# A small product of zeros in each half step of layer 0's attention

## The chip, the cores and the metric

The kernel runs on one core of one Trainium2 chip. Its time is device microseconds of one execution, from the first to the last instruction of the core and what lies around them; lower is better. Times named here are the medians of several runs.

## The reference

Two transformer layers over one sequence of 2048 tokens with 128 channels, in float32. Each layer is a modulated layer norm, attention, a modulated layer norm and a feed-forward part, with gated residuals. Only layer 0's attention is touched by the change:

```python
NHEADS, DK = 16, 8
q = (x @ Wq.T + bq).reshape(b, s, NHEADS, DK)
k = (x @ Wk.T + bk).reshape(b, s, NHEADS, DK)
v = (x @ Wv.T + bv).reshape(b, s, NHEADS, DV)
w = jnp.einsum('bshd,bzhd->bhsz', q, k)
w = w / jnp.sqrt(jnp.float32(DV))
w = jax.nn.softmax(w, axis=-1)
vw = jnp.einsum('bhsz,bzhd->bshd', w, v)
out = vw.reshape(b, s, NHEADS * DV) @ Wo.T + bo
```

There is no mask: every query sees all 2048 keys, in 16 heads of 8 channels. After it come layer 0's experts, layer 1's causal attention, and layer 1's feed-forward part.

## The kernel before

**Units.** Queries are cut into four blocks of 512 (`QB`), keys into 16 tiles of 128, heads into four groups of four (`HG`). A unit is one block of queries with one group of heads: 16 units in layer 0. A bank of PSUM, `av`, holds a unit's weighted sums: 32 partitions for each of the four heads, 512 queries along the row.

**First pass: the maxima.** Softmax needs each query's largest score ahead of the exponential. `first_pass` computes scores with queries on the partitions (L379, a pair of products for two heads, 64 rows of queries and keys split into a high and a low part), and VectorE reduces them to maxima (L383). 32 such steps make a unit. `largest` joins them (L394), splits them in two parts (L404, L405), and `turn` transposes them (L412) and sends them by DMA into spare rows of the query stack.

**Second pass: the exponentials and the weighted sum.** `score` computes the scores again, with keys on the partitions and with the maximum already taken off (L444: the maxima sit in rows of the query stack, which is what `fused` means); ScalarE makes the exponential of two heads at a time (L454), and `weigh` multiplies it with the values (L470: four products, one for each head, in float32, so that each leaves two records in the profile). A unit has 32 half steps, two for each tile of keys: one half step computes scores for two of the four heads, and the weighted sums of half of the queries for all four heads of the tile before.

**Order.** The half steps are written as a generator, `steps`: scores, then `yield`, then one weighted sum. At the `yield` the caller, `look_ahead`, puts in one step of the first pass of the next unit, eight steps (`LEAD`) further ahead. So PE's stream in a half step is: a pair of shifted scores (L444), a pair of scores for the maxima (L379), one weighted sum (L470). `weighing` is the number of the unit whose weighted sum was written last; `other_bank` gives small products the bank that is not in use for it. Instructions are then placed by a scheduler, which may move them within their dependencies unless `keep_in_program_order` holds them.

**Buffers.** Both kinds of scores take their PSUM from one pool, `ps_s`, with three buffers of two banks. They come in turn: an L379 takes the buffer that the exponential of the half step before has read, an L444 the one that a maximum has read. The exponentials lie in five buffers, `ep`.

**Tile forms.** PE's array can be used in parts. The profile shows the part as rows x columns of the weights: 64*128 for L444 and L379, whose two products lie in the upper and the lower 64 rows; 128*32 for L470, whose four lie side by side; 128*128 for transposes and the rest. A float32r product leaves one record, a float32 product two.

Names that the steps use: L501 transposes a unit's sums at its end (`divide`), L528 copies them, L714 and L735 are small products of the expert routing with 16 columns, L230 transposes a layer norm, L450 is layer 1's product that subtracts the maxima (layer 1 is not `fused`), L160 copies a constant at the start.

Of the kernel before, what the change touches and what calls it, by code (L numbers as in the profile page):

```python
# [11 lines left out]
F32R = mybir.dt.float32r  # L12
# [7 lines left out]
P = 128  # L20
# [12 lines left out]
W = 32  # L33
HG = P // W
RT = 64
# [8 lines left out]
def two_layers(ctx: ExitStack, tc: tile.TileContext, a: dict, out: bass.AP):  # L44
    nc = tc.nc
    const = ctx.enter_context(tc.tile_pool(name="const", bufs=1))
# [94 lines left out]
    nc.gpsimd.memset(zeros, 0.0)  # L141
    blank = const.tile([P, P], F32, name="blank")
    nc.gpsimd.memset(blank, 0.0)


    iota = const.tile([P, 32], F32, name="iota")
# [140 lines left out]
    def attention(layer, hT, ngrp, dk, scale, causal, kvp, begin, prepare, wq, bq, folded, ended,  # L287
# [18 lines left out]
        fused = step > 4  # L306
# [4 lines left out]
        with ExitStack() as s:  # L311
# [8 lines left out]
            weighing = -1  # L320
# [105 lines left out]
            def second_pass(u):  # L426


                b, grp = units[u]
                nk = TB * (b + 1) if causal else NT  # L430
                av = banks[u % 2]
                held = {}

                def first_query(kt):
                    return (kt - TB * b) * P if causal and kt >= TB * b else 0

                def score(kt, pair):
                    own = causal and kt >= TB * b
                    q0 = first_query(kt)
                    ps = ps_s.tile([P, 2, QB], F32, name=f"{L}p2_{u}_{kt}_{pair}", tag="s")  # L440
                    for j in range(2):
                        g = 2 * pair + j
                        st, r = grp * nst + g // S, RT * (g % S)
                        nc.tensor.matmul(ps[:, j, q0:], kS(st)[r:r + RT, kt * P:(kt + 1) * P],  # L444
                                         qS[b][r:r + RT, st, q0:], start=True, stop=fused)
                    assert u in shift
                    for j in range(0 if fused else 2):
                        g = 2 * pair + j
                        r = RT * (g % S)
                        nc.tensor.matmul(ps[:, j, q0:], ones[r:r + RT, g // S, :],  # L450
                                         shift[u][r:r + RT, q0:],
                                         start=False, stop=True)
                    e = ep.tile([P, 2, QB], F32, name=f"{L}e_{u}_{kt}_{pair}", tag="e")
                    nc.scalar.activation(e[:, :, q0:], ps[:, :, q0:], AF.Exp, scale=scale)  # L454
                    if own:

                        nc.gpsimd.affine_select(  # L457
                            out=e[:, :, q0:q0 + P], in_=e[:, :, q0:q0 + P],
                            compare_op=ALU.is_ge, fill=0.0, base=0,
                            pattern=[[0, 2], [1, P]], channel_multiplier=-1)  # L460
                    held[kt, pair] = e

                def weigh(kt, c0, c1):
                    nonlocal weighing
                    weighing = u
                    c0 = max(c0, first_query(kt))
                    for g in range(HG):
                        if c0 < c1:

                            nc.tensor.matmul(av[g * W:(g + 1) * W, c0:c1], vA(kt, grp * HG + g),  # L470
                                             held[kt, g // 2][:, g % 2, c0:c1],
                                             start=(kt == 0 and c0 == 0), stop=(kt == nk - 1),
                                             skip_group_check=True)

                def steps():
                    for kt in range(nk):
                        for half in range(2):
                            score(kt, 1 - half)
                            yield
                            if len(weights) > lag:  # L480
                                weights.pop(0)()
                        for half in range(2):
                            weights.append(lambda kt=kt, half=half: weigh(
                                kt, half * QB // 2, (half + 1) * QB // 2))
                    last = weights.pop()
                    weights.append(lambda: (last(), late.extend(normalise(u, av))))

                return steps()

            def normalise(u, av):  # L490
# [717 lines left out]
```

## Time and profile before

| | us |
|---|---|
| median of 3 runs | 1276.62 (1274.73 to 1278.80) |
| the profiled execution | 1279.47 |
| its span, first to last instruction | 1277.8 |
| layer 0's attention, first to last L444 | 91.9 to 815.4 |
| PE, DVE, ACT, POOL busy, of the span | 91%, 74%, 61%, 7% |
| mean granted clock of PE | 0.936 |

PE is TensorE's matmuls, PEld its weight loads, DVE VectorE, ACT ScalarE, POOL GpSimd, SP SyncE. `out<-in` are the program's names of what an instruction writes and reads, then come sizes; xN is the number of instructions joined in a line. In a timeline the first number is the start, the second the duration, in microseconds. The ends of matmuls are modelled, and matmuls overlap in the array, so the time that one of them takes is better read from the starts of two that follow each other than from its duration. A wait is written as who waited, for whom, and then microseconds in total, times, and the longest.

### The profile page before, as it was taken

How to read it: one execution, taken by the hardware profiler on the slowest of the kernel's cores; microseconds unless marked ns; L12 is line 12 of the kernel's file. 1: busy time of each engine (PE TensorE's matmuls, PEld its weight loads, DVE VectorE, ACT ScalarE, POOL GpSimd, SP SyncE). 2: the span in 40 equal slices, each digit the busy share in tenths (PEclk: the TensorE clock that was granted, in tenths of full speed). 3: DMA queues.
4: the chain of work that ended last, by engine and by line, in shares of the span. 5: the costliest groups of instructions: out<-in, count | busy, mean ns of one | idle time of the engine just before them, and what ended most of it. 6: DMA issues, size and time to landing. Idle time of an engine off the chain costs nothing.

```text
span 1277.8 us, 22384 instructions
## 1 busy us (share of the span) xinstructions
PE 1166.8 (91%) x9230; PEld 525.9 (41%) x9230; DVE 946.8 (74%) x1495; ACT 773.1 (61%) x843; POOL 95.2 (7%) x157
## 2 busy tenths in 40 slices
PE   4579999999999999999999999879668999999985
PEld 3233443443344344334344434457433444444432
DVE  4788888889889898988998971342466769888225
ACT  6117777777777777777777777513114435656763
POOL 2011000000000000000000001210411011100113
PEclk9659999999999999999999999979966779999998
DMA  4831010213122024010000000231201101000001
GB/s 127 110 43 34 3 51 6 63 37 106 28 68 68 1 53 115 21 32 2 2 2 2 2 2 9 75 96 52 60 5 33 34 1 34 1 2 1 1 2 33
DMA packets 63095, 45.22 MB, mean 35 GB/s; under 512 B 6609, under 2 KB 56913, under 8 KB 62481
## 3 DMA queue, kind: packets, MB, share of 16 engines
q1 hardware_dynamic: 60224, 40.37, 12.8%
q10 hardware_dynamic: 1744, 1.32, 0.6%
q0 software_dynamic: 1024, 2.10, 0.5%
q8 instruction: 73, 1.20, 0.4%
q14 instruction: 30, 0.24, 0.1%
HBM read 9.88 MB, written 21.95 MB: 25 GB/s over the span
## 4 chain that ended last, share of the span: by engine, by line
PE 80%; DVE 11%; ACT 4%; issue 2%; DMA 1%; POOL 1%; another core or an unknown queue 0%; POOLq 0%; SPq 0%; DVEq 0%; ACTq 0%
PE a0bank L470 23%; PE a0p L444 17%; PE a0p L379 12%; PE a1bank L470 6%; PE a1p L444 4%; DVE a0mx L383 3%; PE a1p L379 2%; PE a1p L450 2%; DVE a1masked L388 2%; DVE a1mx L383 2%; PE sg L941 2%; ACT a0e L454 1%; PE gu L1007 1%; PE a0bank L501 1%; PE a0bank L412 1%
## 5 line engine op out<-in xcount | busy, mean ns | idle before, releaser
L383 DVE TENSOR_REDUCE a0mx<-a0p 128x2 f32<-128x1024 f32 x512 | 623.8, 1224 | 77.3 <-PE a0p L379 67.2
L454 ACT ACTIVATE a0e<-a0p 128x1024 f32<-128x1024 f32 x512 | 522.1, 1024 | 172.9 <-PE a0p L444 148.6
L470 PE MATMUL a0bank<-a0e,vA 128*32 128x256 f32 x4096 | 333.4, 391 | 0.5 <-ACT a0e L454 0.5
L379 PE MATMUL a0p<-kS,a0qS 64*128 64x512 f32 x1024 | 248.1, 481 | 25.9 <-DVE a0mx L383 13.4
L444 PE MATMUL a0p<-a0qS,kS 64*128 64x512 f32 x1024 | 260.7, 498 | 0.0
L454 ACT ACTIVATE a1e<-a1p 128x1024 f32<-128x1024 f32 (+3 forms) x160 | 143.1, 896 | 99.0 <-PE a1p L450 95.7
L444 PEld LDWEIGHTS a0p<-a0qS,kS 64*128 64x128 f32 x1024 | 97.3, 184 | 204.5 <-issue 131.9
L379 PEld LDWEIGHTS a0p<-kS,a0qS 64*128 64x128 f32 x1024 | 100.3, 192 | 110.8 <-ACT a0e L454 56.8
L470 PEld LDWEIGHTS a0bank<-a0e,vA 128*32 128x32 f32 x4096 | 86.4, 108 | 137.6 <-issue 124.4
L383 DVE TENSOR_REDUCE a1mx<-a1p 128x2 f32<-128x1024 f32 x96 | 115.7, 1221 | 29.0 <-PE a1p L379 28.1
L470 PE MATMUL a1bank<-a1e,vA 128*32 128x256 f32 (+1 forms) x1152 | 102.4, 388 | 2.3 <-POOL a1e L457 2.0
L444 PE MATMUL a1p<-a1qS,kS 64*128 64x512 f32 (+3 forms) x320 | 77.1, 474 | 2.5 <-DVE a1mx L388 0.9
L379 PE MATMUL a1p<-kS,a1qS 64*128 64x512 f32 (+3 forms) x320 | 68.5, 432 | 10.3 <-DVE a1mx L388 6.2
L388 DVE CUSTOM_DVE_ANT_0 a1masked<-a1p,later 128x128 f32<-128x128 f32 (+3 forms) x128 | 62.5, 488 | 13.7 <-PE a1p L379 8.7
L759 POOL DMA_INDIRECT sent<-hs,row_i x16 | 16.2, 1011 | 719.2 <-DVE ln11xn L223 689.6
L450 PE MATMUL a1p<-a1mT,a1ones 64*128 64x512 f32 (+3 forms) x320 | 62.6, 384 | 0.7 <-issue 0.7
L444 PEld LDWEIGHTS a1p<-a1qS,kS 64*128 64x128 f32 x320 | 31.8, 193 | 62.6 <-issue 33.4
L379 PEld LDWEIGHTS a1p<-kS,a1qS 64*128 64x128 f32 x320 | 33.1, 204 | 38.8 <-DVE a1mx L388 14.1
L457 POOL TENSOR_SCALAR_AFFINE_SELECT a1e<-a1e 128x256 f32<-128x256 f32 x64 | 26.3, 411 | 253.7 <-ACT a1e L454 253.7
L470 PEld LDWEIGHTS a1bank<-a1e,vA 128*32 128x32 f32 x1152 | 26.3, 109 | 46.0 <-issue 33.3
L413 ACT CAST a0mT<-a0bank 8x512 fp32r<-8x512 f32 x16 | 9.2, 574 | 45.4 <-PE a0bank L412 45.4
L450 PEld LDWEIGHTS a1p<-a1mT,a1ones 64*128 64x128 f32 x320 | 32.7, 199 | 2.3 <-issue 1.8
(342 smaller groups left out, 717.3 us busy)
## 6 DMA issues: line engine op xcount, KB each, us to landing
sent<-blank SPq DMA_DIRECT2D x68, 256.0 KB
kS<-a0qS SPq DMA_DIRECT2D x28, 128.0 KB
wgu_sb<-in_gate_up SPq DMA_DIRECT2D x1, 2048.0 KB
a0qS<-a0qh SPq DMA_DIRECT2D x62, 32.0 KB
a0qS<-a0ql SPq DMA_DIRECT2D x62, 32.0 KB
xs<-sent SPq DMA_DIRECT2D x31, 64.0 KB
y_rows<-y SPq DMA_DIRECT2D x7, 256.0 KB
a1qS<-a1qh SPq DMA_DIRECT2D x24, 64.0 KB
```

Source lines behind the costliest of these rows:

```text
L379: nc.tensor.matmul(ps[:, j, :n], qS[b][r:r + RT, st, i * P:(i + 1) * P], kS(st)[r:r + RT, kb * QB:kb * QB + n], start=True, stop=True)
L383: nc.vector.tensor_reduce(pm[:, i, 2 * pair:2 * pair + 2, kb], ps, AX.X, ALU.max)
L388: nc.vector.tensor_tensor_reduce(masked[:, :n], ps[:, j, :n], later[:, QB - n:], 1.0, LOWEST, ALU.add, ALU.max, pm[:, i, g, kb:kb + 1])
L412: nc.tensor.transpose(ps[:, i * P:(i + 1) * P], nm[:, i, :], ident)
L444: nc.tensor.matmul(ps[:, j, q0:], kS(st)[r:r + RT, kt * P:(kt + 1) * P], qS[b][r:r + RT, st, q0:], start=True, stop=fused)
L450: nc.tensor.matmul(ps[:, j, q0:], ones[r:r + RT, g // S, :], shift[u][r:r + RT, q0:], start=False, stop=True)
L454: nc.scalar.activation(e[:, :, q0:], ps[:, :, q0:], AF.Exp, scale=scale)
L457: nc.gpsimd.affine_select(out=e[:, :, q0:q0 + P], in_=e[:, :, q0:q0 + P], compare_op=ALU.is_ge, fill=0.0, base=0, pattern=[[0, 2], [1, P]] ...
L470: nc.tensor.matmul(av[g * W:(g + 1) * W, c0:c1], vA(kt, grp * HG + g), held[kt, g // 2][:, g % 2, c0:c1], start=(kt == 0 and c0 == 0), sto ...
L501: nc.tensor.transpose(ps[:, i * P:(i + 1) * P], o[:, i * P:(i + 1) * P], ident)
L759: nc.gpsimd.indirect_dma_start(out=sent[t], in_=hs[:, i, :], in_offset=None, out_offset=bass.IndirectOffsetOnAxis(ap=row_i.bitcast(U32)[:, ...
L941: nc.tensor.matmul(ps[:, j, :], w[:, k * P:(k + 1) * P], hT[:, b * QB:(b + 1) * QB], start=True, stop=True)
```

## The change

A constant of zeros, `nothing_r`, 64 x 32, is made at the start. In layer 0 (`fused`), once the unit's first weighted sum has been written (`weighing == u`), each half step adds one product behind the shifted scores: zeros as weights (64 rows, 32 columns), 128 keys of the first stack as the moving side, added to the first 32 partitions and 128 columns of the unit's bank `av`. It adds zero to sums that are being built. `keep_in_program_order` is put around it. Nothing reads it but the sums themselves.

```diff
@@ -141,6 +141,8 @@
     blank = const.tile([P, P], F32, name="blank")
     nc.gpsimd.memset(blank, 0.0)
+    nothing_r = const.tile([RT, W], F32R, name="nothing_r")
+    nc.scalar.copy(nothing_r, blank[:RT, :W])
@@ -476,6 +478,12 @@
                     for kt in range(nk):
                         for half in range(2):
                             score(kt, 1 - half)
+                            if fused and weighing == u:
+                                tc.keep_in_program_order(nc.tensor.matmul(
+                                    av[:W, :P], nothing_r, kS(0)[:RT, :P], start=False,
+                                    stop=False, skip_group_check=True))
                             yield
                             if len(weights) > lag:
                                 weights.pop(0)()
```

With it the lines of the changed kernel stand two further down up to the second edit, and eight further down behind it: L379, L444, L454 and L470 become L381, L446, L456 and L472, and the added product is L484.

## The prediction

> **What bounds the kernel now.** I read the page first, then one table of windows, then PE's timeline for three half steps, then the waits. The page says where the time is:
>
> ```profile
> PE 1166.8 (91%) x9230; PEld 525.9 (41%) x9230; DVE 946.8 (74%) x1495; ACT 773.1 (61%) x843; POOL 95.2 (7%) x157
> ...
> PE 80%; DVE 11%; ACT 4%; issue 2%; DMA 1%; POOL 1%; another core or an unknown queue 0%; POOLq 0%; SPq 0%; DVEq 0%; ACTq 0%
> ```
>
> PE carries 80% of the chain that ended last. The table of windows narrows this to layer 0's attention (first number: PE busy of 600 us; later 1.00: the granted clock):
>
> ```profile
> 100.00:700.00 600.00, 595.35 (x5243) 241.53 (x5236) 537.31 (x559) 448.44 (x457) 1.09 (x1) 1.00 0.13 37
> ```
>
> PE shows 99%, DVE 90%, ACT 75%, and the clock is granted in full, so the change can win no clock there. But ends of matmuls are modelled; what PE's time consists of is read from the starts. Three half steps on PE (start, duration, line, tile form, xcount):
>
> ```profile
> 500.04 0.50 PE L444 MATMUL a0p<-a0qS,kS 64*128 64x512 f32 x2
> 500.37 0.44 PE L379 MATMUL a0p<-kS,a0qS 64*128 64x512 f32 x2
> 500.74 0.64 PE L470 MATMUL a0bank<-a0e,vA 128*32 128x256 f32 x8
> 501.31 0.50 PE L444 MATMUL a0p<-a0qS,kS 64*128 64x512 f32 x2
> 501.72 0.50 PE L379 MATMUL a0p<-kS,a0qS 64*128 64x512 f32 x2
> 502.15 0.64 PE L470 MATMUL a0bank<-a0e,vA 128*32 128x256 f32 x8
> 502.72 0.50 PE L444 MATMUL a0p<-a0qS,kS 64*128 64x512 f32 x2
> 503.06 0.39 PE L379 MATMUL a0p<-kS,a0qS 64*128 64x512 f32 x2
> 503.38 0.42 PE L470 MATMUL a0bank<-a0e,vA 128*32 128x256 f32 x4
> ```
>
> A half step is one pair of shifted scores (L444), one pair of scores for the maxima (L379), one weighted sum (L470: four products, eight records, two passes). From start to start: L444 to L379 0.33, 0.41, 0.34; L379 to L470 0.37, 0.43, 0.32; L470 to the next L444 0.57 always. So a half step takes 1.23 to 1.27 us when nothing is waited for and 1.41 otherwise. Over all of layer 0 the trace's PE starts give the same in the mean: L444 to L379 391 ns (459 of them, one stall of 2.2 us left out), L379 to L470 384 ns, L470 to L444 571 ns. The two groups of quick and slow steps have a cause:
>
> ```profile
> PEld a0p L379 <- ACT a0e L454: 56.8, 219, 0.7
> ```
>
> In 219 half steps the weight load of L379 waits for the exponential (1024 ns on ACT) of the half step before, which holds one of the three PSUM buffers that both score products share. Then its weights cannot be loaded under L444, and L379 takes 0.43 instead of 0.32. So there are two bounds close together: PE's own 1.23 to 1.27 us, and a loop of two half steps through ACT (L444, exponential, L379 of the next half step, L470, L444: 2.68 us from 500.04 to 502.72, 1.34 each).
>
> **The change, part by part.** It adds 464 products: 29 in each of 16 units (the first three half steps of a unit have none), each 64 rows by 32 columns of weights, 128 columns moving, written over the weighted-sum bank. The instruction order of the built program puts 387 of them between an L444 and an L379, 28 between two L470, 49 where PE changes its tile form anyway (in the last unit, which has no maxima left to compute, and before an L379 or a transpose). It has no new wait: its weights and keys have been ready since the start, and its bank is written by PE alone until the unit's end.
>
> Its tile form is 64*32. L444 and L379 both have 64*128, and L470 has 128*32, so 387 times one form is broken in two by another. What a change of form costs, the trace shows: between L470 passes of one form 215 ns go by (431 for two), but from the last one to an L444 309 ns. And an operation that stands alone between other forms:
>
> ```profile
> 771.24 0.50 PE L444 MATMUL a0p<-a0qS,kS 64*128 64x512 f32 x1
> 771.68 0.64 PE L470 MATMUL a0bank<-a0e,vA 128*32 128x256 f32 x8
> ...
> 1034.51 0.63 PE L470 MATMUL a1bank<-a1e,vA 128*32 128x256 f32 x6
> 1035.07 0.33 PE L444 MATMUL a1p<-a1qS,kS 64*128 64x128 f32 x1
> 1035.32 0.44 PE L230 MATMUL a1bank<-ident,ln23xn 128*128 128x128 f32 x2
> ...
> 1070.96 0.33 PE L379 MATMUL a1p<-kS,a1qS 64*128 64x128 f32 x2
> 1071.22 0.62 PE L470 MATMUL a1bank<-a1e,vA 128*32 128x256 f32 x2
> ```
>
> Alone with 512 columns: 0.44 (431 ns in the median of the 13 pairs of L444 between two L470). Alone with 128 columns: 254 to 257 ns. In a row of one form 512 columns take 229 ns (L450 to L379 in layer 1), so standing alone costs 200 ns[...].
>
> [...] No row here has the form 64*32[...]. I take the drain, and the small product's price from the rows.
>
> - The zero product, alone: above, the 254 to 257 ns of the same type and columns with 128 columns of weights (load 183 ns). Below, 186 ns: the products with 16 moving columns (L714, L735) need that from their start to the next form even with their weights loaded ahead. Its own load has 32 columns; L470's loads of 32 take 108 ns, and a first pass with such a load lasts 240 instead of 215. I take 220, near the middle.
> - 387 between L444 and L379: L444 alone 431, zero product 220, L379 alone 431, together 1082 for 391 + 384 = 775 now: +307 each, 118.8 us.
> - 28 between two L470: last pass before another form 309 instead of 215, the product 220, the next first pass 240 instead of 215: +339, 9.5 us.
> - 49 where the form changes anyway: the product alone, 49 x 220 = 10.8 us.
> - Order: in 15 places the transposes of the maxima (L412) now come ahead of a weighted sum and no longer break it. From L379 to the next L444 those places take about 2.08 us now; unbroken, with 431, 585 and 571, 1.59. The transposes also wait for a DVE result (L405, at 264.03 in one unit, transposes at 264.17), so part of it may come back as a wait: 0 to -7 us, taken -4. DVE's small pieces (L404, the layer norm) move by a place or two between maxima; with DVE idle more they cost nothing. SP, POOL and their queues keep their order.
> - ACT gets one copy at the start, 64x32, before the copy L160 (128x128, 280 ns): at most 0.3 us.
>
> Sum: 118.8 + 9.5 + 10.8 - 4 + 0.1 = +135 us. A half step becomes 1.65 us. Then every wait in it is over: the exponential of half step n starts 0.5 to 0.6 us after its L444 and ends by 1.65, while L379 of half step n+1 starts at 1.65 + 0.65; the maximum (1224 ns) has 0.4 us to spare. The cover of the waits, 219 of them, is already in the 775. Nothing waits in line behind the product but PE's own stream.
>
> The profiled execution took 1279.47 us (span 1277.8), 2.9 above the median of 1276.62. On it the sum gives 1414, on the median 1411.6. With 186 ns and -7 the sum is +116, with 257 and no gain from the order +156: 1393 to 1433.
>
> **Rivals.**
> - No drain, because 64*32 lies within the rows and columns of 64*128[...]. Then the product costs [...]the 108 ns that pairs of 128 columns keep in layer 1, and half of the steps hide it in their wait for ACT: 0 to +40 us, 1277 to 1317. Against it: going between 128*32 and 128*128, where also only the columns differ, costs the same 310 ns (L470 to L412).
> - It gets faster. Without a drain the product fills just the time in which L379 waits, and the weights of L379 load under it; a slow step (443 + 431) becomes 337 + 60 + 320. PE's own half step is then 1.29 us against 1.35: 387 x 0.06 = 23 us less, 1253. The point from which it decides: the product must take under 1351 - 1227 = 124 ns of PE's time, 1227 being 336 + 320 + 571. The rows say 186 at least, so I give it little.
> - [...]the granted clock falls under 1.00. At 0.95 some 860 us of PE work would take 43 us more: 1455. No slice in layer 0's attention shows it[...].
> - The product is left out or merged by the build: excluded, the 464 are in the program.
>
> **How the numbers follow.** The drain case 0.84, hidden or nearly so 0.08, faster 0.04, dearer through the clock 0.04. The predicted time is the first case's, 1412. The range is 1365 to 1442: 1393 to 1433, and beyond for a drain that is only partly paid (less by up to some 70 ns a time) or for waits that I don't see. Left out are most of the other three, 0.15, and a tail of the first. A difference of 0.3% is about what a measurement of this kernel can tell. Faster by more: 0.05; within: 0.03; slower: 0.92.
>
> **What would show it right or wrong.** In the profile of the changed kernel[...]: right if L446 to L484 takes about 431 ns, L484 to L381 186 to 257, L381 to L472 about 431 with hardly a quick one left, L472 to L446 still 571; the wait of L381's weight loads for ACT is gone, and DVE and ACT are busy about 76% and 63% of layer 0's attention. Wrong if L446 to L484 takes 336 (no drain ahead of it), if L381's weights are loaded under L484, or if the granted clock is under 1.00 there.

## The result, and the profile after

The changed kernel takes 1299.0 us in the median of four runs (1291.36 to 1304.6), the kernel before 1277.25 beside it: a ratio of 1.0153, 95% interval 1.0124 to 1.0183, or +16 to +23 us. The forecast of 1412 us and its whole range missed: slower, but by a sixth of what I had worked out. The number fits the first rival, that there is no drain. A drain is here a name for a gap in the traces: two products which follow each other on PE stand as far apart as if each were alone (0.43 us behind a pair of scores, not 0.34). What the array does in that time no run shows.

The same lines of the page as were shown of the kernel before:

```profile
PE 1174.7 (90%) x9694; PEld 553.3 (43%) x9694; DVE 947.4 (73%) x1495; ACT 774.4 (60%) x844; POOL 95.2 (7%) x157
...
PE 74%; DVE 17%; ACT 5%; issue 2%; DMA 1%; POOL 1%; another core or an unknown queue 1%; ACTq 0%; POOLq 0%; DVEq 0%
```

There are 464 more products (9694 against 9230), yet PE's busy time grew by only 8 us. The table of windows for the same 600 us:

```profile
100.00:700.00 600.00, 589.39 (x5503) 261.99 (x5499) 525.77 (x548) 438.55 (x446) 2.92 (x1) 1.00 0.14 37
```

DVE is at 88% and ACT at 73%, where I had said 76% and 63% should stand. So the half steps hardly got longer. PE's timeline shows them:

```profile
507.70 0.64 PE L472 MATMUL a0bank<-a0e,vA 128*32 128x256 f32 x8
508.27 0.50 PE L446 MATMUL a0p<-a0qS,kS 64*128 64x512 f32 x2
508.61 0.22 PE L484 MATMUL a0bank<-kS,nothing_r 64*32 64x128 f32 x1
508.62 0.50 PE L381 MATMUL a0p<-kS,a0qS 64*128 64x512 f32 x2
509.04 0.64 PE L472 MATMUL a0bank<-a0e,vA 128*32 128x256 f32 x8
509.61 0.50 PE L446 MATMUL a0p<-a0qS,kS 64*128 64x512 f32 x2
```

From start to start, L446 to L484 takes 0.34 us, as L444 to L379 did without a wait; the product and L381 start within 10 ns of each other here (6 ns in the median of layer 0); L381 to L472 takes 0.43, L472 to L446 0.57. Every half step is 1.34 us now. Before, they were by turns about 1.23 and 1.41, 1.34 in the mean. Told by the exponentials of half steps 14 to 24 of the units 1 to 13, two half steps take 2.680 us before and 2.691 after in the mean (2.680 and 2.683 in the median). The waits in the changed kernel:

```profile
PEld a0p L381 <- ACT a0e L456: 16.6, 54, 0.7
```

L381's weights wait for ACT 54 times instead of 219. That much of the forecast came true, but not because the steps became long.

The two profiled spans differ by 20.2 us. The starts of layer 0's 512 exponentials tell where they lie (differences are of the unrounded times):

| stretch | before, us | after, us | difference |
|---|---|---|---|
| up to the first exponential | 94.5 | 96.3 | +1.8 |
| units 0 to 14 | 676.0 | 690.1 | +14.0 |
| unit 15 | 46.3 | 51.9 | +5.6 |
| from there to the last weighted sum | 2.2 | 2.6 | +0.4 |
| all that follows | 458.8 | 457.1 | -1.7 |

In a common unit (ten of them) the difference is 0.82 us, and 0.65 of it lies in two half steps near the unit's start. Units 4, 8 and 12 lose 1.35 to 1.94.

### The profile page after: what moved, and what is told of

It is laid out like the page before. It is cut to its first block, busy times and chain, and to the rows that moved or that the text cites. A ratio compares the mean times of both kernels' runs of the same rounds, so it can differ in the third digit from the quotient of the medians.

```text
span 1298.0 us, 23317 instructions
## 1 busy us (share of the span) xinstructions
PE 1174.7 (90%) x9694; PEld 553.3 (43%) x9694; DVE 947.4 (73%) x1495; ACT 774.4 (60%) x844; POOL 95.2 (7%) x157
## 4 chain that ended last, share of the span: by engine, by line
PE 74%; DVE 17%; ACT 5%; issue 2%; DMA 1%; POOL 1%; another core or an unknown queue 1%; ACTq 0%; POOLq 0%; DVEq 0%
PE a0bank L472 20%; PE a0p L446 15%; PE a0p L381 10%; DVE a0mx L385 7%; PE a1bank L472 6%; PE a1p L446 4%; PE a1p L381 2%; PE a1p L452 2%; PE a0bank L484 2%; DVE a1masked L390 2%; ACT a0e L456 2%; DVE a1mx L385 2%; PE sg L949 2%; PE gu L1015 1%; PE a1bank L267 1%
## 5 line engine op out<-in xcount | busy, mean ns | idle before, releaser
L456 ACT ACTIVATE a0e<-a0p 128x1024 f32<-128x1024 f32 x512 | 522.6, 1024 | 193.9 <-PE a0p L446 173.4
L472 PE MATMUL a0bank<-a0e,vA 128*32 128x256 f32 x4096 | 333.0, 395 | 0.3
L381 PE MATMUL a0p<-kS,a0qS 64*128 64x512 f32 x1024 | 266.9, 481 | 24.8 <-DVE a0mx L385 13.4
L446 PE MATMUL a0p<-a0qS,kS 64*128 64x512 f32 x1024 | 259.3, 502 | 2.1 <-DVE a0mx L385 2.1
L456 ACT ACTIVATE a1e<-a1p 128x1024 f32<-128x1024 f32 (+3 forms) x160 | 143.1, 896 | 93.0 <-PE a1p L452 89.7
L446 PEld LDWEIGHTS a0p<-a0qS,kS 64*128 64x128 f32 x1024 | 96.5, 185 | 209.7 <-issue 179.9
L381 PEld LDWEIGHTS a0p<-kS,a0qS 64*128 64x128 f32 x1024 | 120.3, 193 | 91.2 <-DVE a0mx L385 31.6
L472 PEld LDWEIGHTS a0bank<-a0e,vA 128*32 128x32 f32 x4096 | 81.8, 109 | 120.5 <-issue 110.8
L472 PE MATMUL a1bank<-a1e,vA 128*32 128x256 f32 (+1 forms) x1152 | 101.5, 386 | 2.3 <-POOL a1e L459 2.0
L484 PE MATMUL a0bank<-kS,nothing_r 64*32 64x128 f32 x464 | 103.6, 223 | 0.0
L446 PE MATMUL a1p<-a1qS,kS 64*128 64x512 f32 (+3 forms) x320 | 75.5, 463 | 3.2 <-DVE a1mx L385 1.0
L381 PE MATMUL a1p<-kS,a1qS 64*128 64x512 f32 (+3 forms) x320 | 66.5, 421 | 10.9 <-DVE a1mx L390 6.3
L446 PEld LDWEIGHTS a1p<-a1qS,kS 64*128 64x128 f32 x320 | 31.2, 188 | 63.2 <-issue 34.1
L484 PEld LDWEIGHTS a0bank<-kS,nothing_r 64*32 64x32 f32 x464 | 49.6, 107 | 17.7 <-issue 17.7
L381 PEld LDWEIGHTS a1p<-kS,a1qS 64*128 64x128 f32 x320 | 32.1, 198 | 37.8 <-DVE a1mx L390 13.0
L472 PEld LDWEIGHTS a1bank<-a1e,vA 128*32 128x32 f32 x1152 | 26.2, 109 | 45.1 <-issue 32.3
```

Of the source, the lines that this page charges most:

```text
L381: nc.tensor.matmul(ps[:, j, :n], qS[b][r:r + RT, st, i * P:(i + 1) * P], kS(st)[r:r + RT, kb * QB:kb * QB + n], start=True, stop=True)
L484: tc.keep_in_program_order(nc.tensor.matmul(av[:W, :P], nothing_r, kS(0)[:RT, :P], start=False, stop=False, skip_group_check=True))
```

## The experiments

Three theories stood at the start. A: there is no drain between 64*128 and 64*32; the product costs PE some 0.1 us a half step, which is paid out of the wait for ACT; the loss comes from the unit's start. B: every product costs the same 47 ns. C: PE or DVE, not the loop through ACT, sets the pace. Ratios are to the kernel before, measured beside each run.

**Where the loss lies.** Three kernels split the 464 products by place (the comments name the run):

```diff
-                            if fused and weighing == u:
+                            if fused and weighing == u and kt > 2 and u + 1 < len(units):    # e1_steady
+                            if fused and weighing == u and kt <= 2 and u + 1 < len(units):   # e2_first
+                            if fused and weighing == u and u + 1 == len(units):              # e3_last
```

(kt counts from 0, so kt > 2 begins with the fourth tile of keys, where the expectation says third. The numbers of products in it are right.)

**e1_steady**

> The added product only from the third tile of keys on and not in the last unit: 390 of the 464, 382 of them between an L446 and an L381. Theory A (no drain between 64*128 and 64*32; the product runs beside L381 and takes only the loading ahead of L381's weights; in the steady half steps that is paid out of a wait, because the pace is set by the loop of two half steps through ACT, 2.68 us): +0 to +6 us, 1277 to 1283. Theory B (every one of the 464 products costs the same 47 ns, 21.7 us over 464): +18 us, 1295.

Measured: ratio 1.0021 (0.9998 to 1.0045), +2.7 us for 390 products. A holds; B's 18 us are out.

**e2_first**

> The added product only in the first three half steps that can have it, in all units but the last: 45 of the 464, 25 of them between two weighted sums, 12 between a weighted sum and a pair of maxima scores. Theory A: these change the tile form of L472 and pay for it, about 0.7 us a unit as the traces of before and after show in the starts of the exponentials: +8 to +12 us, 1285 to 1289. Theory B: 45 x 47 ns = +2 us, 1279.

Measured: 1.0086 (1.0072 to 1.0100), +11 us, for 45 products. A holds, B is out.

**e3_last**

> The added product only in the last unit: 29 of the 464. Theory A: there are no maxima scores beside which it could run, PE's order around the routing changes and PE waits: +4 to +8 us, 1281 to 1285. Theory B: 29 x 47 ns = +1.4 us, 1278.5.

Measured: 0.9986 (0.9956 to 1.0015), no loss beyond the noise. A's 4 to 8 us are out; B's 1.4 lies within the interval. In the profiles unit 15 takes 45.8 us here and 45.1 in e1_steady and e2_first, which have no product there (46.3 in the kernel before). L446 to L472 takes 487 ns with a product in between and 432 without, 55 each. So the 5.6 us of unit 15 in the changed kernel are not the price of its products. What differs is the granted clock (the column behind POOL's). The first line is the window of unit 15 of the changed kernel, the second the same order of products in e10_free, a run further below, the third a part of the first:

```profile
786.00:841.00 55.00, 54.04 (x438) 23.05 (x438) 11.27 (x47) 37.55 (x43) 11.84 (x12) 0.88 0.05 15
```

```profile
787.00:836.00 49.00, 47.91 (x438) 21.42 (x436) 11.28 (x47) 37.76 (x44) 11.83 (x12) 1.00 0.05 17
```

```profile
824.10:837.60 13.50, 13.50 (x80) 4.64 (x79) 1.57 (x6) 6.01 (x6) 3.83 (x4) 0.50 0.06 21
```

These are the same 438 records of PE at a mean of 0.88 and at 1.00; the 0.88 is a stretch of 13.7 us at 0.50. Up to it the half steps of unit 15 are those of e10_free, and from there on they take 6.2 us more. The changed kernel's four runs also go by their mean clock: 1291.36 us at 0.942, 1298.24 at 0.933, 1299.76 at 0.934, 1304.60 at 0.926. Why the clock falls in some executions is open; no run here was made to tell.

What e2_first pays for is seen on PE's timeline at the start of unit 9, in the kernel before and then in the changed kernel:

```profile
507.63 0.50 PE L444 MATMUL a0p<-a0qS,kS 64*128 64x512 f32 x2
508.06 1.50 PE L470 MATMUL a0bank<-a0e,vA 128*32 128x256 f32 x24
509.50 0.51 PE L379 MATMUL a0p<-kS,a0qS 64*128 64x512 f32 x2
```

```profile
518.53 0.50 PE L446 MATMUL a0p<-a0qS,kS 64*128 64x512 f32 x2
518.96 0.64 PE L472 MATMUL a0bank<-a0e,vA 128*32 128x256 f32 x8
519.53 0.24 PE L484 MATMUL a0bank<-kS,nothing_r 64*32 64x128 f32 x1
519.70 0.64 PE L472 MATMUL a0bank<-a0e,vA 128*32 128x256 f32 x8
520.27 0.24 PE L484 MATMUL a0bank<-kS,nothing_r 64*32 64x128 f32 x1
520.45 0.64 PE L472 MATMUL a0bank<-a0e,vA 128*32 128x256 f32 x8
521.02 0.24 PE L484 MATMUL a0bank<-kS,nothing_r 64*32 64x128 f32 x1
521.02 0.52 PE L381 MATMUL a0p<-kS,a0qS 64*128 64x512 f32 x2
```

Three weighted sums in a row took 1.44 us and take 2.06 with two products between them: 0.31 each. Here the change of form is paid: 0.57 instead of 0.43 ahead of the product, then 0.17 to 0.18 for it. The third product, ahead of L381, costs next to nothing (L381 to L472 takes 0.46 instead of 0.43). The 25 places of e2_first between two weighted sums make 7.8 us; its units 0 to 14 are 8.7 us longer in the profile.

**Which form drains.**

```diff
-    av[:W, :P], nothing_r, kS(0)[:RT, :P], start=False,
+    av[:W, :P], nothing_r, kS(0)[:, :P], start=False,        # e4_128x32, nothing_r 128 x 32
+    av[:, :P], nothing_r, kS(0)[:RT, :P], start=False,       # e5_64x128, nothing_r 64 x 128
+    av[:W, :P], blank[:RT, :W], kS(0)[:RT, :P].bitcast(F32), start=False,   # e11_float32_64x32
+    av[:, :P], blank[:RT, :], kS(0)[:RT, :P].bitcast(F32), start=False,     # e12_float32_64x128
```

**e4_128x32**

> The same zero product with 128 rows of zeros and keys instead of 64, so its tile form is 128*32 instead of 64*32; number and places are unchanged. Theory A1 (the array drains when the number of rows of the form changes, not when only the columns do): L446 to L484 431 ns, the product alone some 180 to 220, L381 alone 431, +0.29 us in 387 half steps, about 1390. Theory A2 (small products between the scores never drain, whatever the form): as the changed kernel, 1295 to 1303.

Measured: 1.0961 (1.0905 to 1.1016), 1405 us. PE's timeline:

```profile
500.71 0.50 PE L446 MATMUL a0p<-a0qS,kS 64*128 64x512 f32 x2
501.13 0.25 PE L484 MATMUL a0bank<-kS,nothing_r 128*32 128x128 f32 x1
501.31 0.50 PE L381 MATMUL a0p<-kS,a0qS 64*128 64x512 f32 x2
501.74 0.64 PE L472 MATMUL a0bank<-a0e,vA 128*32 128x256 f32 x8
502.31 0.50 PE L446 MATMUL a0p<-a0qS,kS 64*128 64x512 f32 x2
```

From start to start 0.43, 0.18, 0.43, 0.57: a half step of 1.61 us. A1's gaps are there, for this float32r product; that a change of the columns alone never drains, e11_float32_64x32 below does not bear out. But for the product's own 0.18 it is the half step that I forecast (431, 220, 431, 571), for another form. By an estimate from unit 0 some 9 us of the time are the clock's: the granted clock stays at 0.50 until 124 us of the span (in the kernel before until 101), and unit 0 takes 61.3 us against 52.2 in the next.

**e5_64x128**

> The same zero product with 128 columns of zeros instead of 32, so its tile form is 64*128, that of the scores, and it adds zeros to all 128 partitions of the bank. Theory A: if 64*32 between 64*128 costs no drain, this one behaves alike: L446 to L484 337 ns, steady pace 1.34 us or up to 0.08 more for the longer load of weights (183 ns instead of 107): 1295 to 1330. If 64*32 did cost something of its own, this one would be faster than the changed kernel by more than 5 us.

Measured: 1.0148 (1.0099 to 1.0197); two half steps take 2.693 us, against 2.691 with the form 64*32, which so costs no more between the scores than their own form.

**e11_float32_64x32**

> The same zero product in the same places with the same tile form 64*32, but in float32 instead of float32r: two passes of 128 columns, some 108 ns each by the passes of L470 (216 ns for 256 columns). Theory D (64*32 is free between 64*128 because it is float32r; a float32 product[...] drains, as going between 128*32 and 128*128 does): L446 to L484 431 ns, L381 alone 431, half step 1.70 us or more, 1410 or more. Theory E (what drains is a change of the rows, and 64 rows stay 64 whatever the type): L446 to L484 337, half step 1.34 + 0.11 to 0.16, about 1340 to 1365.

Measured: 1.1691 (1.1619 to 1.1762), 1500 us. The two records of the product are its two passes:

```profile
501.75 0.50 PE L446 MATMUL a0p<-a0qS,kS 64*128 64x512 f32 x2
502.18 0.40 PE L484 MATMUL a0bank<-kS,blank 64*32 64x128 f32 x2
502.51 0.50 PE L381 MATMUL a0p<-kS,a0qS 64*128 64x512 f32 x2
502.94 0.64 PE L472 MATMUL a0bank<-a0e,vA 128*32 128x256 f32 x8
503.51 0.49 PE L446 MATMUL a0p<-a0qS,kS 64*128 64x512 f32 x2
```

The same form in the same place, in float32: 0.43 ahead of it, 0.33 for it, 0.43 behind, 1.76 us in all. Theory D holds; E's 337 ns ahead of it are out. Of the 216 us that the ratio makes, some 36 are the clock's, by the same estimate: it stays at 0.50 until 192 us of the span, and unit 0 takes 93.2 us against 56.7 in most others.

**e12_float32_64x128**

> The control of the run before: float32 again, with 128 columns of zeros, tile form 64*128 as the scores. Theory D: no drain, 1340 to 1370, at least 40 us under the 64*32 product in float32. Theory E: within 15 us of the 64*32 product in float32. If a change from float32r to float32 drained by itself, both would stand above 1400.

Measured: 1.0499 (1.0432 to 1.0567), 1351 us; L446 to L484 takes 338 ns and the half step 1.455 us in the median. So it is not the change of type that drains. Theory D holds: between products of 64*128 a product of 64*32 drains in float32 (432 ns behind the pair before it) and not in float32r (338).

**Who sets the pace, and what the product costs PE.**

```diff
-  nc.scalar.activation(e[:, :, q0:], ps[:, :, q0:], AF.Exp, scale=scale)
+  q1 = QB // 2 if fused else QB
+  nc.scalar.activation(e[:, :, q0:q1], ps[:, :, q0:q1], AF.Exp, scale=scale)
...
-  held[kt, g // 2][:, g % 2, c0:c1],
+  held[kt, g // 2][:, g % 2, 0:c1 - c0] if fused else held[kt, g // 2][:, g % 2, c0:c1],
```

**e7_halfexp_before**

> The kernel before, with layer 0's exponential made over 256 of its 512 columns for each head (both halves of the weighted sums read the same 256 columns): half of the exponentials are left out, PE and DVE have the same work. Theory A (the loop through ACT sets the steady pace): the exponential takes about 0.55 us instead of 1.02, the loop falls to about 2.2 us, the pace to PE's own 1.23 or DVE's 1.26: 390 x 0.08 = -31 us, about 1245; the waits of L379's weight loads for ACT are gone. Theory C (PE or DVE sets the pace): within 5 us of 1277.

Measured: 0.9665 (0.9629 to 0.9701), -43 us, more than the 31 of theory A, since the half step fell to PE's own 1.23. PE's timeline:

```profile
521.34 0.50 PE L444 MATMUL a0p<-a0qS,kS 64*128 64x512 f32 x2
521.67 0.40 PE L379 MATMUL a0p<-kS,a0qS 64*128 64x512 f32 x2
522.00 0.64 PE L471 MATMUL a0bank<-a0e,vA 128*32 128x256 f32 x8
522.57 0.50 PE L444 MATMUL a0p<-a0qS,kS 64*128 64x512 f32 x2
```

The steady half steps take 1.23 us, with PE's work unchanged. A holds: the loop through ACT set the pace of the kernel before.

**e8_halfexp_after**

> The changed kernel with the same half of layer 0's exponentials left out. Theory A (with the product PE's own stream is 1.34 us a half step, as long as the loop through ACT): the pace stays 1.34, the time stays within 8 us of the changed kernel, about 1295; the product then costs some 50 us against the kernel with half of the exponentials and no product, which is its true price on PE, 0.1 us each. Theory C (the product costs PE nothing between the scores, only at the units' ends): 22 us more than without the product, about 1267.

Measured: 1.0083 (1.0050 to 1.0115).

```profile
520.38 0.50 PE L446 MATMUL a0p<-a0qS,kS 64*128 64x512 f32 x2
520.72 0.39 PE L381 MATMUL a0p<-kS,a0qS 64*128 64x512 f32 x1
520.72 0.22 PE L486 MATMUL a0bank<-kS,nothing_r 64*32 64x128 f32 x1
520.78 0.44 PE L381 MATMUL a0p<-kS,a0qS 64*128 64x512 f32 x1
521.15 0.64 PE L473 MATMUL a0bank<-a0e,vA 128*32 128x256 f32 x8
521.72 0.50 PE L446 MATMUL a0p<-a0qS,kS 64*128 64x512 f32 x2
```

1.34 us again, with half of ACT's work gone; the time is some 9 us under the changed kernel's by the ratios, a little more than A allowed. The median half step is 1.233 without the product and 1.339 with it where ACT no longer matters, so the product costs PE 106 ns. In total that is 1.0083 - 0.9665, or 53 us, as A has it. The changed kernel pays 20, because it had a wait of the same size to put it in.

Where the 106 ns go: L381 to L472 took 326 ns in e7_halfexp_before and takes 430 here. The weight loads (PEld, timeline of the changed kernel) show a part of it:

```profile
524.73 0.19 PEld L446 LDWEIGHTS a0p<-a0qS,kS 64*128 64x128 f32 x2 [0.41 <-issue]
524.84 0.11 PEld L484 LDWEIGHTS a0bank<-kS,nothing_r 64*32 64x32 f32 x1
525.07 0.19 PEld L381 LDWEIGHTS a0p<-kS,a0qS 64*128 64x128 f32 x2
```

The product's load goes ahead under L446. The two loads of L381 begin in this half step only with the product itself, at 525.07. In the kernel before both go ahead, by more than 20 ns, in 213 of 415 half steps of layer 0 (L379 to L470 takes 327 ns in the median) and neither in 201 (431 ns). In the changed kernel one goes ahead in 214 of 370 and neither in 156, and from the first of L381 and the product to L472 it takes 432 and 436 ns; in e8_halfexp_after one of the two still goes ahead in nearly every half step, and L381 to L472 takes 430 ns all the same. e9_behind below tells the two parts of the price from each other.

**e6_two**

```diff
+    (the added product stands twice)
```

> Two zero products, one behind the other, in each half step that had one. Theory A (the steady half step of the changed kernel has 1.34 us of PE and 1.34 us of the loop through ACT, so the slack is used up): the second product costs its own time on PE, 60 to 110 ns, in full: 464 x 0.06 to 0.11 = +28 to +51 on the changed kernel, 1327 to 1350. Theory B (each product costs the same 47 ns): 1299 + 22 = 1321.

Measured: 1.0379 (1.0339 to 1.0419), 1331 us. The median half step is 1.397 us: the second product costs 57 ns, and in full, since no wait is left to take it. A's number holds, at its low end; B's, 10 us lower, is not excluded by this run's time alone.

**e9_behind**

```diff
                             score(kt, 1 - half)
-                            (the added product)
                             yield
+                            (the added product)
```

> The added product stands behind the step of the first pass instead of ahead of it: 368 of the 464 between an L381 and an L472. Theory A (what it costs PE in a half step is the loading ahead of L381's weights, about 0.1 us): that loading comes back, L446 to L381 is 337 ns without a wait, L381 to L472 320 to 430 plus what the product adds between two forms that drain anyway (0 to 60 ns), so the steady pace stays at 1.34 us and the time is within 10 us of the changed kernel, 1285 to 1305. If place between the score products were what matters, against the drain at L472: a product that stands last before the change of form costs 186 to 220 ns by the rows of L714 and of L446 with 128 columns, 368 x 0.15 = +55 us, 1330.

Measured: 1.0284 (1.0232 to 1.0336), 1309 us; between the two forecasts, and neither. A half step without a wait:

```profile
512.63 0.50 PE L446 MATMUL a0p<-a0qS,kS 64*128 64x512 f32 x2
512.97 0.39 PE L381 MATMUL a0p<-kS,a0qS 64*128 64x512 f32 x2
513.20 0.21 PE L485 MATMUL a0bank<-kS,nothing_r 64*32 64x128 f32 x1
513.34 0.64 PE L472 MATMUL a0bank<-a0e,vA 128*32 128x256 f32 x8
513.91 0.50 PE L446 MATMUL a0p<-a0qS,kS 64*128 64x512 f32 x2
```

Where both loads of L381 went ahead, L381 to L472 takes 383 ns in the median (134 half steps), against 326 in the kernel before: the product costs 57 ns here, as the second one does in e6_two, and PE's own half step is 1.29 us. So the product itself is some 57 of the 106 ns, and the other 49 are left for the load of L381 that no longer goes ahead. That is a difference of two places, and no run takes the load alone. The pace did not become faster than the loop through ACT for it: the half step is 1.347 in the median of all. Most of the loss against the changed kernel is around the transposes of the maxima: half steps 24 and 25 together take 1.2 us more than there in each common unit.

**e10_free**

```diff
-    tc.keep_in_program_order(nc.tensor.matmul(...))
+    nc.tensor.matmul(...)
```

> The changed kernel without the holding of the product in program order (the number of products and their neighbours on PE are the same, 387 between scores). Theory A: within 5 us of the changed kernel, 1294 to 1304. If the holding costs (other instructions that are held in order, or the scheduler's room): nearer to the kernel before, 1285 or less.

Measured: 1.0132 (1.0086 to 1.0177). Its units 0 to 14 take 690.9 us, against 690.1 in the changed kernel. The holding costs nothing that can be told from noise.

## Why the prediction was wrong

**The step that failed is the sum's first term**, "387 between L444 and L379 ... +307 each, 118.8 us". I forecast 431 + 220 + 431 = 1082 ns from L444 to L470 in place of 775. In the changed kernel the means are 339 + 5 + 430 = 774: next to nothing was added. The pace of the steady half steps rose by 5 ns at most (2.691 against 2.680 us for two), and e1_steady, 382 of whose products stand there, lost 2.7 us.

Two assumptions in that term were wrong. **The first is the drain.** I took "no row here has the form 64*32" and carried the rows of the other forms over to it. The rows were right for what they showed: e4_128x32 drains in this very place (0.43 us), and so does 64*32 in float32 (0.43). But the added product is float32r, and its 64*32 does not drain between two 64*128 (0.34). Without a drain the product costs PE 106 ns, some 57 of them its own. (That e4's 1405 us come so near to my 1412 is in part luck: its product is shorter than I took it, and some 9 us, by the estimate from unit 0, are the clock's.) The evidence that I gave against the rival ("between 128*32 and 128*128, where also only the columns differ") is from a float32 product, L470 (310 ns to L412); the type was the difference that I didn't look at. The rival's number was right, but not the reason that it gave: in e11_float32_64x32 the form lies within the same rows and columns and drains (0.43 us ahead of it).

Why the type decides, no run here shows.

**The second is the base.** I added the product to a mean half step that held 219 waits, and let all waits vanish in a step of 1.65 us. With a product of 106 ns PE's own half step is 1.339 us against the loop's 1.340: the product just fills the wait. I had both bounds, 1.23 to 1.27 and 1.34, and a decisive point, but used them only for the rival of a gain. (That point, 124 ns, is mis-added: by its own terms, 391 + 384 + 571 less 1227, it is 119.) There the size was right, since 106 ns fit under it. A gain could not follow: the loop through ACT held the half step at 1.34 us in the kernel before, with 1.23 to 1.27 of PE's own, and at 1.347 in e9_behind, with 1.29.

**The 28 between two weighted sums** were right in size, 0.31 us measured for 0.34 forecast, by two errors that go against each other: the change of form took 0.14 us instead of 0.12, the product 0.17 to 0.18 instead of 0.22.

**The 49 where the form changes anyway**, 10.8 us, were priced too high. 26 of them stand in the last unit; where they lie between L446 and L472 they cost PE 55 ns each instead of 220, and the unit took some 0.7 us longer. Another 12 stand ahead of L381 at the units' starts and cost next to nothing.

**The order.** The transposes moved as told, but from L381 to the next L446 those places take 1.97 us instead of 2.03, some -0.8 us in all where I took -4. The wait that I had named took most of the rest: PE waits for L407 (L405 before) in 14 places, 4.6 us. And "DVE's small pieces ... cost nothing" failed in units 4, 8 and 12. There three pieces of the layer norm stand between two maxima, where it was one or two before, and three L446 in a row wait for a buffer (PE's timeline, changed kernel, unit 8):

```profile
484.00 0.50 PE L446 MATMUL a0p<-a0qS,kS 64*128 64x512 f32 x2 [0.20 <-DVE a0mx L385]
...
485.59 0.50 PE L446 MATMUL a0p<-a0qS,kS 64*128 64x512 f32 x2 [0.19 <-DVE a0mx L385]
...
487.19 0.50 PE L446 MATMUL a0p<-a0qS,kS 64*128 64x512 f32 x2 [0.18 <-DVE a0mx L385]
```

These three units together lose about 2.2 us beyond a common unit's 0.82 each. A half step is 1.60 us here. In the 1.65 us that I forecast DVE would have had the room; in 1.34 it had not.

**The clock.** I gave the rival of a lower clock little. In two kernels it counted: in e4_128x32 and e11_float32_64x32, which drain between the scores, the granted clock came up to 1.00 some 20 and 90 us later than in the kernel before (101 us of the span), and in none of the others more than 10. Why, no run here tells.

**What stays open.** The ratios of the three parts, +0.21%, +0.86% and -0.14%, make some 12 us; the changed kernel lost 16 to 23. In the profiles the parts do add up: units 0 to 14 are 4.6 us longer in e1_steady and 8.7 in e2_first, 13.3 of the 14.0. The 5.6 us of unit 15 are the stretch at half clock. That the changed kernel's other executions lost to the clock too is argued from four mean clocks, not shown, and what makes the clock fall is open.

## What to carry to other kernels

Find out what sets the pace of a loop before pricing an addition to one of its engines. An engine that shows 99% busy could hold a wait of 0.1 us a step here; what was added up to that size was nearly free (+2.7 us for 390 products in e1_steady), and what came beyond it was paid in full (57 ns a half step for the second product of e6_two). Before a price read from one operation is carried over to another, compare form and data type: the same 64*32 stood 338 ns behind a pair of scores in float32r and 432 in float32. When an added instruction makes a scheduler reorder another engine, count that engine's slack in the new step: pieces of DVE that moved cost some 2.2 us here.

## What the runs showed of the hardware

- A float32r product of 64*32 between pairs of 64*128 starts 338 ns behind the pair before, and the next pair 6 ns behind it (medians of the changed kernel). In float32 the same product stands 432 ns behind the pair before, and the next pair 332 ns behind it (e11_float32_64x32). Of the form 64*128 it stands 338 ns behind the pair before in float32 (e12_float32_64x128), and in float32r two half steps take 2.693 us (e5_64x128), against 2.691 with 64*32.
- Between weighted sums of 128*32, where the number of rows changes too, the same float32r product of 64*32 costs 0.31 us (changed kernel, unit 9).
- A float32r product of 64*32 with 128 moving columns costs PE 106 ns between two pairs of scores (half steps of 1.233 us in e7_halfexp_before, 1.339 in e8_halfexp_after). Behind the second pair it costs 57 (e9_behind), and so does a second product (e6_two); the remaining 49 are put down, by difference, to a weight load of the next pair that no longer goes ahead.
- The granted clock of one and the same stretch, the last unit with 98% of PE busy, was 1.00 in one kernel's execution (e10_free) and 0.88 in another's (the changed kernel), which held 13.7 us at 0.50. In e11_float32_64x32 it stayed at 0.50 from 100 to 180 us of the span with PE shown busy all the while.
